# Where the sampling weights' loads stand in SyncE's queue: start of a half band or middle of the one before

## The chip, the cores and the metric

The kernel runs on one core of a Trainium2 chip. The metric is the device time of one execution in microseconds. Before the change the median of three runs was 9661.97 us (9661.39 to 9698.82). A core has five engines with instruction streams of their own: TensorE (PE: matmuls, and PEld for its weight loads), VectorE (DVE), ScalarE (ACT), GpSimd (POOL) and SyncE (SP), which here only issues DMAs. An engine works off its stream in order; a waiting instruction holds up all that follows it on that engine. DMAs are issued by SyncE, by ScalarE's queue and by GpSimd's queue, and run on 16 DMA engines.

## The reference

Thirty-two images of 96 channels by 56 by 56 go through two layers in float32.

- Layer one is an inverted bottleneck: a 1x1 convolution to 576 hidden channels, a 3x3 depthwise convolution, a squeeze-and-excite gate, a 1x1 convolution back to 96, and the input added.
- Layer two computes channel and spatial gates from Fourier magnitudes, multiplies them in (`y`), and then runs a deformable convolution. What matters here is its sampling:

```python
offset = _conv(aux, off_w, off_b, (1, 1))
off = offset.reshape(b, 9, 2, h, w)
px = xx + off[:, :, 0]
py = yy + off[:, :, 1]
sampled = _grid_sample_taps(y, px, py)
y_def = jnp.einsum('bcthw,oct->bohw', sampled, def_w.reshape(c, c, 9))
z = (1 - gate) * y_base + gate * y_def
```

For every pixel and each of nine taps, `_grid_sample_taps` interpolates `y` bilinearly at a fractional place. At the end `z` is normalised over the batch, and `relu(zn + x)` is returned.

## The kernel before

**Tiling.** An image is cut into 7 bands of 8 rows (`NBD`), a band into two half bands of 7 tile pairs (`NTH`). Bilinear sampling is done as a matmul: each 4x4 tile of outputs sees a block of 8x8 = 64 pixels (`NS`), and for each output and tap there is a column of 64 weights, the product of a row hat and a column hat. `block_channels` (line 696) turns the blocks so that pixels lie on partitions; `sample_tiles` (713) multiplies them by the weights (the matmul of line 721, 28 recorded per half band); `pack` (729) and `deform` (735) apply the deformable convolution's own weights.

**The weights' way.** For band n, `offsets` (641) lets TensorE compute the offsets, VectorE copies them to `at` (651), GpSimd's queue stores them as `od` (655), SyncE loads them eight-fold as `ht` (667), ScalarE makes the hats (670, 671), and ScalarE's queue stores them as `hd` in HBM (674). It is a generator of 16 steps spread over one band, two bands ahead of use: `find(n + 2)` runs beside band n, and its store of `hd` is its last step, at that band's end. For each half band `weights_load` (678) then loads from `hd`, with copies, the column hats `wc` and the row hats `wr`: four DMAs of 252 KB each on SyncE (lines 685 and 686, twice). `weights` (690) multiplies them on VectorE in place, 128 x 1008 numbers (line 692): "the product". The pool of `wc` has three buffers, that of `wr` two.

**The main loop** (line 1105) runs over all 224 bands of all images; its half bands are numbered m = 2n + h here. In each half band it

1. issues the loads of half band m + 1 (`prepare`, line 1117; `READY` and `AHEAD` are 1 each, so it asks for loads up to number m + 1),
2. takes the finished weights and blocks of m and samples the first group of three tile pairs,
3. calls `pump()` for each, which moves on two streams of other images: `first` (the bottleneck's hidden layer: taps on VectorE at line 261, xt loads at line 212) and `second` (projection with hq loads at line 305, Fourier magnitudes with x loads at line 361),
4. ends the half band before (`deform`), issues the product of m + 1 (line 1131) and turns blocks,
5. samples the second group of four tile pairs, pumping again, and packs.

At a band's end it pumps three times more and refills rows of `y` (loads of lines 584 and 596).

**What sets the order.** Line 1351 puts SyncE under manual order: it issues its DMAs exactly in the order of the program. For the other engines the framework's planner decides: it reckons when each instruction's inputs will be ready and fills each engine's stream accordingly, earlier program places first. So a changed place of a load in the program changes SyncE's order directly, and may change the planned order of the others.

Of the kernel before, what the change touches and what calls it, by code (L numbers as in the profile page):

```python
# [64 lines left out]
AHEAD = 1  # L65
READY = 1
# [611 lines left out]
def weights_load(nc, p, hd, h):  # L678

    src = hd.rearrange("n i t k -> n i (t k)")[:, :, h * NTH * KP : (h + 1) * NTH * KP]  # L680
    wc = p["wc"].tile([2 * NS, NTH * KP], FP, name="wc")
    wr = p["wr"].tile([2 * NS, NTH * KP], FP, name="wr")
    for s in range(2):
        ps = slice(s * NS, (s + 1) * NS)
        nc.sync.dma_start(wc[ps], src[2 * s].unsqueeze(0).to_broadcast([SB, SB, NTH * KP]))
        nc.sync.dma_start(wr[ps], src[2 * s + 1].unsqueeze(1).to_broadcast([SB, SB, NTH * KP]))
    return wc, wr


def weights(nc, wc, wr):  # L690

    nc.vector.tensor_tensor(wc, wc, wr, ALU.mult)  # L692
    return wc


def block_channels(nc, p, yp, j, h):

    yt = p["yt"].tile([2 * NS, NTH, C], FP, name="yt")
    yb = p["ybl"].tile([C, NTH, 2, SB, SB], FP, name="ybl")
    src = yp[:C, j * RB : j * RB + SB, h * NTH * TS : h * NTH * TS + SB]  # L700
    for s in range(2):
        blocks = bass.AP(src.tensor, src.offset + s * TS * WY, [src.ap[0], [TS, NTH], [WY, SB], [1, SB]])
        nc.gpsimd.tensor_copy(yb[:, :, s], blocks)  # L703
    for lo, hi in ((0, 4), (4, NTH)):
        pt = bank(p)
        for t in range(lo, hi):
            nc.tensor.transpose(pt[:, (t - lo) * C : (t - lo + 1) * C], yb[:, t].rearrange("c s r x -> c (s r x)"),  # L707
                                p["w"]["ident"][:C, :C])
        nc.scalar.copy(yt[:, lo:hi].rearrange("p t c -> p (t c)"), pt[:, : (hi - lo) * C])  # L709
    return yt  # L710


def sample_tiles(nc, p, yt, s, v, group):


    pts = [(bank(p), bank(p)) for _ in group]
    for (lo, hi), pt in zip(group, pts):
        for t in range(lo, hi):
            for k in range(2):
                ps = slice(k * NS, (k + 1) * NS)  # L720
                nc.tensor.matmul(pt[k][:C, (t - lo) * KP : (t - lo + 1) * KP], yt[ps, t], s[ps, t * KP : (t + 1) * KP],  # L721
                                 start=True, stop=True)
    for (lo, hi), pt in zip(group, pts):
        for k in range(2):
            nc.scalar.copy(v[:C, :, lo:hi, k].rearrange("c k t p -> c t k p"),  # L725
                           pt[k][:C, : (hi - lo) * KP].rearrange("c (t k p) -> c t k p", t=hi - lo, k=NTAP))


def pack(nc, v):

    for i in range(3):
        nc.scalar.copy(v[C:, 1 + 2 * i : 3 + 2 * i], v[i * QC : (i + 1) * QC, KA:])  # L732
# [25 lines left out]
def gates_of(nc, p, hid):  # L758

    pgs = bank(p), bank(p)  # L760
    for i, pg in enumerate(pgs):
        ps = slice(i * NS, i * NS + DMID)
        nc.tensor.matmul(pg[:C, :BW], p["w"]["dg2p"][ps], hid[ps], start=True, stop=True)
    return [gate_from(nc, p, pg) for pg in pgs]
# [174 lines left out]
def layers(tc, a, dp, x1d, zd, stats, far):  # L939
# [8 lines left out]
    with ExitStack() as ctx:  # L948
# [29 lines left out]
        def flush():  # L978
            while later:
                later.pop(0)[1]()  # L980
# [27 lines left out]
        def start(b, length):  # L1008
            streams[:] = [[second(b + 1), 0, n_second, slot + 3, slot + length - 8],
                          [first(b + 2), 0, n_first, slot, slot + length]]  # L1010

        def pump():
            nonlocal slot
            slot += 1
            for st in streams:
                due = st[2] * min(1.0, (slot - st[3]) / (st[4] - st[3]))
                while st[1] < due:
                    st[1] += 1
                    next(st[0], None)
            later.sort(key=lambda e: e[0])  # L1020
            while later and later[0][0] <= slot:
                later.pop(0)[1]()

        def drain():
            for st in streams:
                for _ in st[0]:
                    pass
# [3 lines left out]
        def refill(b, upto):  # L1031

            upto = min(H, upto)
            r = filled.get(("y", b), 0)
            while ("sa", b) in p and r < upto:
                r1 = min(upto, r + RB)
                args = load_rows(nc, p, yp, b, x1d[b], r, r1)
                later.append((slot + 4, lambda args=args: attend_rows(nc, p, b, *args)))
                r = filled["y", b] = r1
            r = filled.get(("fq", b), 0)  # L1040
            if ("fq", b) in p and r < upto:
                load_freq(nc, p, yp, b, r, upto)
                filled["fq", b] = upto
# [11 lines left out]
        def end_half(n, h, v, gate, st):  # L1055
            if h == 0:
                pds[n] = p["pd"].tile([128, 512], FP, name="pd")
            deform(nc, p, pds[n], v, h)
            if h:
                pd = pds.pop(n)  # L1060
                later.append((slot + 2, lambda: join(n, pd, gate, st)))
# [14 lines left out]
        def find(n):  # L1076
            if n % 2 == 0:
                hids.append(p["hid"].tile([2 * NS, BW], FP, name="hid"))
            hid = hids[n // 2][n % 2 * NS : n % 2 * NS + DMID]
            return offsets(nc, p, yp, bands[n][1], top[:, n % NBD : n % NBD + 1], hid, ybs, hds)  # L1080
# [11 lines left out]
        def prepare(upto):  # L1092

            nonlocal n_loads
            while n_loads < min(upto, 2 * len(hds)):
                n, m = divmod(n_loads, 2)
                loads.append(weights_load(nc, p, hds[n], m))
                n_loads += 1
# [6 lines left out]
        for n, (b, j) in enumerate(bands):  # L1105
            if j == 0:
                st = p["st"].tile([C, NBD, 6], FP, name="st")
            if j == turn:
                drain()
                refill(b + 1, j * RB - PD)  # L1110
                flush()
                start(b + 1, slots)
            more = find(n + 2) if n + 2 < len(bands) else iter(())
            next(more, None)
            for h in range(2):
                v = p["vp"].tile([128, NTAP, NTH, 2, TP], FP, name="v")
                prepare(2 * n + h + READY + AHEAD)
                s = ready.pop(0)
                yt = yts.pop(0)
                for i, group in enumerate(GROUPS):  # L1120
                    sample_tiles(nc, p, yt, s, v, group)
                    for _ in range(group[0][0], group[-1][1]):
                        next(more, None)
                        pump()
                    if i == 0:
                        for end in ends:
                            end()
                        ends.clear()
                        if h == 1 and n + 1 < len(bands):
                            yts.append(block_channels(nc, p, yp, bands[n + 1][1], 0))  # L1130
                        ready.extend(weights(nc, *ws) for ws in loads[:1])
                        del loads[:1]
                        if h == 0:
                            yts.append(block_channels(nc, p, yp, j, 1))
                pack(nc, v)
                if h == 0:
                    if n % 2 == 0:
                        gates.extend(gates_of(nc, p, hids[n // 2]))
                    gate = gates.pop(0)
                ends.append(lambda n=n, h=h, v=v, gate=gate, st=st: end_half(n, h, v, gate, st))  # L1140
            for _ in more:
                pass
            pump()
            pump()
            pump()
            if b + 1 < B:
                refill(b + 1, (j + 1) * RB - PD if j < NBD - 1 else H)
            if j == NBD - 1:
                nc.vector.tensor_reduce(top[:, NBD:], top, AX.X, ALU.max)
# [350 lines left out]
```

## Time and profile before

| what | value |
|---|---|
| median of the runs | 9661.97 us |
| profiled execution | 9648.5 us (span 9646.7 us) |
| main loop | about 430 to 9358 us of the span, 448 half bands, 19.9 us each |
| TensorE, share busy / granted clock over the span | 88% / 0.923 |
| VectorE, ScalarE, GpSimd busy | 75%, 55%, 26% |
| DMA traffic | 1485.98 MB, 154 GB/s in the mean |
| product of weights (line 692) | 448 times, 1.26 us in the mean |
| loads wc and wr (lines 685, 686) | 896 each, 252 KB each |
| issue of one of these loads on SyncE | 0.57 to 0.60 us |

How to read the profile's lines: a group line gives line number, engine, operation, what it writes and reads, how often, then busy us and the mean in ns, then the idle time of the engine just before these instructions and what ended it. A wait line reads "who <- what it waited for: us in total, times, longest us". The same view for SyncE's queue shows how long the queue stood before an issue. A timeline line gives the start in us, the duration, the engine (a q for an issue by its queue), line, operation, and in brackets the idle time before it with what ended it. A line of busy time by stretch gives the stretch, its length, busy us of PE, PEld, DVE, ACT and POOL with instruction counts, TensorE's granted clock, the DMA engines' busy share, and GB/s.

### The profile page before, as it was taken

What the parts mean: (1) busy time and instruction counts of PE and PEld (TensorE: products, weight loads), DVE (VectorE), ACT (ScalarE), POOL (GpSimd) and SP (SyncE); (2) the same over time, 40 slices, a digit from 0 to 9 for tenths busy, and PEclk for the clock granted to TensorE, in tenths of its full rate; (3) what the DMA queues carried; (4) which work ended last, traced back from release to release, by engine and by line L of the source; (5) the groups of instructions that cost most, each with busy time, mean ns of one, the idle gap of its engine ahead of it and who ended that gap; (6) DMA issues with size and microseconds to landing.
All of it is one profiled execution on the core that took longest, in us unless ns stands there. A gap on an engine that the chain in (4) does not pass through costs nothing. (4 is left out here: it accounts for less than half of the span.)

```text
span 9646.7 us, 129705 instructions
## 1 busy us (share of the span) xinstructions
PE 8472.7 (88%) x48374; PEld 5064.2 (52%) x48374; DVE 7227.2 (75%) x6948; ACT 5322.1 (55%) x10262; POOL 2532.6 (26%) x2642
## 2 busy tenths in 40 slices
PE   6889989998999999999899989999999999999870
PEld 3455555555555555555555555555555555555540
DVE  7688777778777787877777887777878777777323
ACT  2355555565555556555555655555555555565453
POOL 1123223222222322222232322233222323322210
PEclk9899999999999999999999999999999999999985
DMA  2355555555555555555555555555555555554449
GB/s 94 95 143 148 151 152 160 150 149 143 147 155 154 160 154 145 145 149 155 154 160 155 145 142 153 151 158 154 153 139 145 150 157 157 153 152 135 130 154 417
DMA packets 1069473, 1485.98 MB, mean 154 GB/s; under 512 B 590438, under 2 KB 840086, under 8 KB 1056550
## 3 DMA queue, kind: packets, MB, share of 16 engines
q1 hardware_dynamic: 858747, 985.20, 37.9%
q10 hardware_dynamic: 153803, 329.80, 9.2%
q0 software_dynamic: 56288, 162.60, 6.7%
q8 instruction: 388, 6.36, 0.3%
q14 instruction: 247, 2.02, 0.1%
HBM read 1064.29 MB, written 412.65 MB: 153 GB/s over the span
## 5 line engine op out<-in xcount | busy, mean ns | idle before, releaser
L261 DVE SCALAR_TENSOR_TENSOR acch<-hp,w,acch 128x1512 f32<-128x1512 f32 (+1 forms) x2250 | 4320.5, 1920 | 32.8
L605 PE MATMUL mm<-yp,c_jointW 104*128 104x448 f32 x4032 | 1649.0, 561 | 9.0 <-ACT yt L709 5.5
L740 PE MATMUL pd<-v,c_def 128*96 128x224 f32 (+1 forms) x6272 | 1414.8, 376 | 127.6 <-ACT v L732 104.1
L703 POOL COPY ybl<-yp 96x448 f32<-96x448 f32 x896 | 1014.7, 1159 | 1903.7 <-PE mm L707 1903.3
L721 PE MATMUL mm<-wc,yt 64*96 64x144 f32 x12544 | 1168.1, 308 | 153.5 <-DVE yb L638 76.8
L740 PEld LDWEIGHTS pd<-v,c_def 128*96 128x96 f32 (+1 forms) x6272 | 1051.8, 173 | 437.4 <-ACT v L732 142.5
L168 PE MATMUL mm<-xt,w 96*128 96x392 f32 (+3 forms) x2688 | 1136.3, 561 | 133.8 <-ACT yt L709 96.0
L605 PEld LDWEIGHTS mm<-yp,c_jointW 104*128 104x128 f32 x4032 | 783.6, 196 | 806.0 <-issue 762.6
L721 PEld LDWEIGHTS mm<-wc,yt 64*96 64x96 f32 x12544 | 884.2, 167 | 489.8 <-issue 188.0
L221 ACT ACTIVATE acch<-acch,sh,inv 128x1568 f32<-128x1568 f32 x288 | 487.5, 1693 | 1159.0 <-DVE acch L261 1143.9
L692 DVE TENSOR_TENSOR wc<-wc,wr 128x1008 f32<-128x1008 f32 x448 | 564.6, 1260 | 704.2 <-DMA wr<-hd 690.5
L725 ACT COPY v<-mm 96x288 f32<-96x288 f32 (+1 forms) x2688 | 1003.6, 442 | 117.7 <-PE mm L721 78.9
L172 ACT ACTIVATE hp<-mm,sh,inv 128x392 f32<-128x392 f32 (+2 forms) x1216 | 811.8, 672 | 326.9 <-PE mm L168 282.1
L633 PE MATMUL mm<-yp,c_base0W 96*64 96x448 f32 x4032 | 913.5, 550 | 0.0
L323 PE MATMUL mm<-hq,w3s 128*96 128x392 f32 x2048 | 788.2, 531 | 127.4 <-DMA hq<-h2d 125.9
L655 POOL DMA_DIRECT2D od<-at x224 | 186.3, 832 | 2275.1 <-DVE at L651 1451.9
L732 ACT COPY v<-v 32x448 f32<-32x448 f32 x1344 | 755.3, 562 | 30.3
L168 PEld LDWEIGHTS mm<-xt,w 96*128 96x128 f32 (+1 forms) x2688 | 389.9, 189 | 495.1 <-issue 264.8
L709 ACT COPY yt<-mm 128x384 f32<-128x384 f32 (+1 forms) x896 | 350.9, 441 | 491.5 <-PE mm L707 489.4
L323 PEld LDWEIGHTS mm<-hq,w3s 128*96 128x96 f32 x2048 | 336.3, 173 | 477.7 <-issue 382.5
L466 POOL TENSOR_TENSOR o<-o,xc 96x392 f32<-96x392 f32 x256 | 396.5, 1549 | 643.9 <-ACT o L333 642.3
L633 PEld LDWEIGHTS mm<-yp,c_base0W 96*64 96x64 f32 x4032 | 294.6, 134 | 515.5 <-issue 490.2
(194 smaller groups left out, 9023.7 us busy)
## 6 DMA issues: line engine op xcount, KB each, us to landing
h2d<-acch ACTq DMA_DIRECT2D x288, 784.0 KB
wc<-hd SPq DMA_DIRECT2D x896, 252.0 KB
wr<-hd SPq DMA_DIRECT2D x896, 252.0 KB
hq<-h2d SPq DMA_DIRECT2D x128, 980.0 KB
hq<-h2d SPq DMA_DIRECT2D x128, 784.0 KB
x<-x1d SPq DMA_DIRECT2D x768, 98.0 KB
ht<-od SPq DMA_DIRECT2D x224, 252.0 KB
hd<-ht ACTq DMA_DIRECT2D x224, 252.0 KB
```

The lines of the kernel that those rows point to most:

```text
L168: nc.tensor.matmul(pt[p0 : p0 + w1.shape[1], : rows * W], w1, xts[hf][:, r0 * W : (r0 + rows) * W], start=True, stop=True)
L172: nc.scalar.activation(h1[lo:hi, row0 : row0 + rows, 1 : 1 + W], pt[lo:hi, : rows * W].rearrange("p (h w) -> p h w", h=rows), AF.Silu, bia ...
L261: nc.vector.scalar_tensor_tensor(acc[:, lo:hi], win, wk, acc[:, lo:hi], ALU.mult, ALU.add)
L323: nc.tensor.matmul(pts[half][:C, :EW], w3s[:, ch], hq, start=(i == 0), stop=False)
L605: nc.tensor.matmul(view, weights[:, k], yp[:channels, r0 : r0 + RB, dx + PD - 1 : dx + PD - 1 + W], start=(k == 0), stop=(k == NTAP - 1))
L633: nc.tensor.matmul(pb[k % 2 * BC : (k % 2 + 1) * BC, :BW].rearrange("p (h w) -> p h w", h=RB), w["base"][:, k], yp[:C, r0 : r0 + RB, dx + ...
L692: nc.vector.tensor_tensor(wc, wc, wr, ALU.mult)
L703: nc.gpsimd.tensor_copy(yb[:, :, s], blocks)
L721: nc.tensor.matmul(pt[k][:C, (t - lo) * KP : (t - lo + 1) * KP], yt[ps, t], s[ps, t * KP : (t + 1) * KP], start=True, stop=True)
L725: nc.scalar.copy(v[:C, :, lo:hi, k].rearrange("c k t p -> c t k p"), pt[k][:C, : (hi - lo) * KP].rearrange("c (t k p) -> c t k p", t=hi - ...
L732: nc.scalar.copy(v[C:, 1 + 2 * i : 3 + 2 * i], v[i * QC : (i + 1) * QC, KA:])
L740: nc.tensor.matmul(out.rearrange("c q (t x) -> c t q x", x=TS), p["w"]["def"][ks, k], v[ks, k].rearrange("c t s (r x) -> c t (s r) x", r=T ...
```

## The change

The call of `prepare` moves from the start of a half band to its middle, right after the product, and asks for one half band more. At that place in half band m the loads of m + 2 are issued; before, they were issued at the start of half band m + 1. In the program's order the four loads thereby pass what SyncE is given in the second sampling group of m, at the end of a band, and nothing else. The number of loads, their sizes and the buffers are the same; `prepare` still stops at the bands whose `hd` has been written in the program.

```diff
             for h in range(2):
                 v = p["vp"].tile([128, NTAP, NTH, 2, TP], FP, name="v")
-                prepare(2 * n + h + READY + AHEAD)
                 s = ready.pop(0)
                 yt = yts.pop(0)
                 for i, group in enumerate(GROUPS):
@@
                             yts.append(block_channels(nc, p, yp, bands[n + 1][1], 0))
                         ready.extend(weights(nc, *ws) for ws in loads[:1])
                         del loads[:1]
+                        prepare(2 * n + h + 1 + READY + AHEAD)
                         if h == 0:
                             yts.append(block_channels(nc, p, yp, j, 1))
```

## The prediction

> **What bounds the kernel now.** I read the page first (busy shares, costliest groups), then the waits of all engines, the waits of SyncE's own queue, busy time by stretch for the main loop, and the timelines of SyncE, VectorE and TensorE for one image (5019 to 5301 us).
>
> ```profile
> PE 8472.7 (88%) x48374; PEld 5064.2 (52%) x48374; DVE 7227.2 (75%) x6948; ACT 5322.1 (55%) x10262; POOL 2532.6 (26%) x2642
> L692 DVE TENSOR_TENSOR wc<-wc,wr 128x1008 f32<-128x1008 f32 x448 | 564.6, 1260 | 704.2 <-DMA wr<-hd 690.5
> ...
> DVE wc L692 <- DMA wr<-hd: 690.5, 152, 18.3
> PE mm L323 <- DMA hq<-h2d: 125.9, 31, 9.4
> PE mm L386 <- POOL x L366: 34.3, 32, 4.0
> ...
> SPq L361 <- PE mm L386: 1272.9, 144, 52.9
> SPq L667 <- DMA od<-at: 777.1, 83, 15.1
> SPq L685 <- DMA hd<-ht: 702.6, 42, 24.3
> SPq L361 <- DMA x1d<-o: 650.4, 34, 22.0
> ...
> 430.00:9358.00 8928.00, 8172.23 (x47211) 4896.05 (x47209) 6833.02 (x6363) 5105.56 (x9959) 2486.46 (x2576) 0.94 0.54 149
> 5078.00:5111.00 33.00, 24.40 (x123) 14.34 (x117) 20.53 (x18) 16.51 (x34) 2.67 (x2) 0.74 0.36 108
> ```
>
> TensorE bounds the main loop: 8172.2 us busy of 8928, so 755.8 us idle is all that better timing can win, plus what the clock loses (granted 0.94 in the loop, so 0.06 x 8928 = 536 us of clock). VectorE waits 690.5 us for the landing of wr, 152 times, more than for anything else. SyncE's queue spends most of its time waiting: it issues in program order and stands before x loads, ht loads and the weights' loads, so what stands in front of a load sets its time.
>
> The timelines show how (SyncE five lines, VectorE two, TensorE two):
>
> ```profile
> 5033.76 2.82 SPq L361 DMA_DIRECT2D x<-x1d  x6
> 5036.62 0.59 SPq L685 DMA_DIRECT2D wc<-hd  x1
> ...
> 5074.72 0.66 SPq L667 DMA_DIRECT2D ht<-od  x1
> 5075.48 0.57 SPq L685 DMA_DIRECT2D wc<-hd  x1
> 5276.74 9.08 SPq L305 DMA_DIRECT2D hq<-h2d  x2
> ...
> 5047.31 1.21 DVE L692 TENSOR_TENSOR wc<-wc,wr 128x1008 f32<-128x1008 f32 x1 [5.50 <-DMA wr<-hd]
> 5089.44 1.21 DVE L692 TENSOR_TENSOR wc<-wc,wr 128x1008 f32<-128x1008 f32 x1 [8.73 <-DMA wr<-hd]
> ...
> 5091.90 0.74 PE L707 MATMUL mm<-c_ident,ybl 96*128 96x96 f32 x3 [6.19 <-ACT sq L413]
> 5289.26 3.57 PE L323 MATMUL mm<-hq,w3s 128*96 128x392 f32 x7 [3.01 <-DMA hq<-h2d]
> ```
>
> The reader is to see two kinds of late loads. The product at 5047.31 waits for loads that were issued at 5036.62 because six x loads stood before them until 5033.76, waiting for a store of x1d. The product at 5089.44 waits for loads issued at 5075.48 behind an ht load that waited for od; TensorE then idles 6.19 us, released over ScalarE's squares and VectorE.
>
> **The change, part by part.**
>
> *What moves.* Nothing is added or removed: 448 sets of four loads, 0.57 to 0.60 us each to issue, 2.5 us a set. The set for half band m goes from the start of half band m-1 to the middle of m-2, right after the product for m-1. On SyncE it passes just what the streams and the refill issue in the second sampling group: by the program's order some 662 x loads (L361), 180 hq loads (L305), 248 yp loads and 93 frequency rows (L584, L596) and 58 xt loads (L212), over the whole run. It does not pass the ht load (L667), which is issued in the first group. The POOL and ScalarE queues keep their issues.
>
> *Gain on VectorE.* In the image shown the products wait 5.5 (5047.31), 8.7 (5089.44), 5.5 (5240.1) and 2.0 us (5286.0), 21.7 in all; 690.5 / 32 images is 21.6, so it is typical. Before three of the four stand x or hq loads, which the set now passes; there it can be issued 13 to 20 us sooner than before (from the queue's last issue before its new place, and from hd's landing), more than the stall. Before the fourth (8.7) stands the ht load: that stall stays. So 13.0 of 21.7, 60% or about 414 us of VectorE's waits, go.
>
> *What of it reaches TensorE.* I followed each TensorE gap of the loop back over its releasers to the last TensorE instruction: 304 us (155 gaps) pass a landing of wr. 184 us of these are in the fourth half band of the images (the 6.19 us is one), behind the stall that stays. 120 us are elsewhere. Those cannot give more than 120, and give nothing if the ScalarE copies that release TensorE next (rows L725, L732, L709 in its waits) are as late. I take 85: next late are those copies, and they queue behind VectorE's work only in part.
>
> *Clock.* Idle TensorE costs clock beside: 536 us lost for 755.8 idle, 0.7 us per us; in the stretch 5078 to 5111 8.6 us idle and a clock of 0.74. The gaps that go are shorter than that one, so I take half of 0.7: 85 x 0.35 = 30, bounds 0 and 60. [...]
>
> *Cost: who stands behind the set now.* A set that must wait holds SyncE. Sets for even m need hd, stored by ScalarE near the end of the band before (landing 2.6 us after its issue where SyncE waited for it). One place per image gets a hold of some 23 us: the set at 5105.39 already waits for hd, and the xt load before it (5081.81) will now stand behind. I cost this at nothing: xt is loaded some 100 us before its use, and TensorE waited for xt only at the kernel's start (33.2 us); without that cover it would be up to 23 us per image. Elsewhere hd holds the queue 0 to 3 us. x loads behind the set come 2.5 us later and share its transfer; TensorE and POOL wait little for x now (34.3 us, and 17.9 for x's landing): I take +15, bounds 0 and +52, a doubling. The waits on buffers are not new: wc of m is free when m-3 was sampled, wr when product m-2 ran, both before the new place but for one place per image where hd holds longer anyway and one with 4.5 us.
>
> *hq.* The last hq quarter makes TensorE wait 125.9 us. The load issued at 5276.74 lands 12.5 us later, with a set (5271.1 to 5273.7) in front of it; after the change that set has gone 13 us earlier. But the next set is then issued between the two hq loads (5277 and 5285.5), and the second lands later. Bounds -126 and +256 (8 us in each of 32 images); the two pull opposite ways, I take 0.
>
> *Order on the other engines.* Only SyncE follows the program; for the others a planner, which reckons when data land, sets the order, and it will plan anew. The trace cannot show this. Bounds: -60 (a third of the 184 us behind the stall that stays) and one more stall like that of 5089.44 per image, 6.2 us x 31 = +192 without clock. I take +20, near the small end, since in most half bands VectorE is over 85% busy (17.96 of 18 us in the half band at 5204) and leaves little room to move a product.
>
> *Sum.* -85 - 30 + 15 + 0 + 20 = -80 us. The profiled execution took 9648.5 us (span 9646.7), so 9568; the median of the runs, 9661.97, is 13.5 above the profiled one, so 9582.
>
> **The rivals.**
>
> *A. Forecast:* the stalls at x and hq loads go, 9582 (0.8% faster), its own range 9480 to 9613. For it: nothing but SyncE's waiting loads stood before those sets.
>
> *B. The stall moves with the product (slower).* The planner sees the loads land sooner and puts the product as much earlier on VectorE; where it reckons the landing too early, VectorE stands again. For it: that happened in the fourth half band, where the product ran half a half band ahead of its place in the program, 11.3 us after its last load was issued, and stalled 8.7. Against: in most half bands VectorE is too full. Price: one more such place per image, 6.2 us of TensorE plus 0.7 of it in clock = 10.5 us x 31 = 326, less the 80 won: 9908; in half of the images: 9745. It decides from about 2.6 us of new TensorE idle per image on (80 / 31), if the products' lead falls below 12 us. [...]
>
> *C. The second hq load of the last quarter is late (slower).* Set between the hq loads: +256 - 126 + the -80 above = +50, 9710. It decides if that hq load lands over 6 us later than now. Against: the set may have landed by then.
>
> *D. No change.* VectorE's stalls go, but TensorE waits as long for the ScalarE copies: 0 reaches it, costs +15 + 20: 9697, range 9615 to 9710. For it: TensorE's idle rows name ScalarE in the main, VectorE's product itself 7.7 us.
>
> **How the numbers follow.** A measurement of this kernel can tell about 0.5% from no change (48 us; the runs span 37). A 0.50, B 0.16, C 0.13, D 0.21. Faster by over 0.5%: A but for its edge, 0.48. Within: D and edges, 0.22. Slower: B, C, 0.30. The predicted time is A's, 9582. The range: down to 9430 (the full 120 with 60 of clock, and half of hq's 126: 9419, rounded in), up to 9800 (C, and B in up to two thirds of the images); beyond lie the rest of B and a planner's luck.
>
> **What the changed profile would show.** Right: VectorE's wait for wr at 250 to 320 us, most of it in the fourth half band; the sets behind x and hq loads 13 us or more sooner; TensorE idle in the loop near 670 us; clock 0.94 to 0.95. B: that wait at 500 us or more, products earlier than now against the sampling that uses them. C: the row of L323 waiting for hq over 200 us. D: wr's row down and TensorE's idle still about 750. What would make it wrong above all: a new order on ScalarE or VectorE that delays the copies TensorE waits for, which no row of this trace shows.

## The result and the profile after

The changed kernel takes 9817.83 us in the median (9809.00 to 9838.04) against 9676.99 us of the kernel before beside it: a ratio of 1.0147, 95% interval 1.0117 to 1.0177, some 142 us slower. 9582 was predicted, and the measured time lies above the range's upper end, 9800. Of these last 18 us, 15 are the base's: the median of the kernel before was 9661.97 over three runs and 9676.99 with the fourth. The profiled execution took 9838.04 us (span 9836.2).

From the page of the changed kernel (busy time, and the group of the product):

```profile
PE 8601.3 (87%) x48374; PEld 5139.0 (52%) x48374; DVE 7286.7 (74%) x6948; ACT 5325.8 (54%) x10264; POOL 2446.4 (25%) x2642
...
L692 DVE TENSOR_TENSOR wc<-wc,wr 128x1008 f32<-128x1008 f32 x448 | 563.5, 1258 | 738.8 <-DMA wr<-hd 726.5
```

From the waits of its engines (us in total, times, longest us):

```profile
DVE wc L692 <- DMA wr<-hd: 726.5, 221, 18.8
...
ACT yb L628 <- DVE at L651: 434.5, 129, 9.0
...
PE mm L721 <- DVE yb L638: 192.1, 89, 6.7
...
PE mm L386 <- POOL x L366: 171.2, 57, 7.9
...
PE mm L323 <- DMA hq<-h2d: 12.8, 6, 7.2
```

In the kernel before, ScalarE's wait for VectorE's `at` was:

```profile
ACT yb L628 <- DVE at L651: 128.0, 70, 5.2
```

From the waits of the changed kernel's SyncE queue:

```profile
SPq L685 <- DMA hd<-ht: 1566.2, 131, 27.3
...
SPq L361 <- DMA x1d<-o: 316.6, 30, 14.0
```

And the changed kernel's busy time over the main loop:

```profile
430.00:9545.00 9115.00, 8297.47 (x47188) 4969.92 (x47186) 6892.63 (x6362) 5107.76 (x9958) 2400.73 (x2576) 0.92 0.54 146
```

The stall that was to go has not gone: the product waits 726.5 us for wr instead of 690.5, and 221 times instead of 152. The hq wait is gone (125.9 to 12.8). SyncE waits less behind x1d (650.4 to 316.6) and more than twice as long for hd (702.6 to 1566.2). TensorE's idle time in the loop is 9115.00 - 8297.47 = 817.5 us, 62 more than before, and its busy time has grown by 125 at a lower clock (0.94 to 0.92).

What happened is plainest in one half band, the eleventh of an image (number 10, counted 0 to 13). VectorE, ScalarE and TensorE of the changed kernel, from its timelines (brackets: idle before, and what ended it):

```profile
5627.85 1.21 DVE L692 TENSOR_TENSOR wc<-wc,wr 128x1008 f32<-128x1008 f32 x1 [4.13 <-DMA wr<-hd]
5629.10 0.69 DVE L651 COPY at<-mm 18x224 f32<-18x224 f32 x2
...
5629.82 0.63 ACT L628 ACTIVATE yb<-mm,c_cvec 32x448 f32<-32x448 f32 x1 [3.62 <-DVE at L651]
...
5630.50 0.48 PE L721 MATMUL mm<-wc,yt 64*96 64x144 f32 x2 [0.38 <-ACT yb L628]
5631.25 0.73 PE L721 MATMUL mm<-wc,yt 64*96 64x144 f32 x6 [0.27 <-ACT hp L172]
5632.42 0.73 PE L721 MATMUL mm<-wc,yt 64*96 64x144 f32 x8 [0.44 <-DVE yb L638]
```

The same place in the kernel before:

```profile
5501.54 1.21 DVE L692 TENSOR_TENSOR wc<-wc,wr 128x1008 f32<-128x1008 f32 x1 [1.01 <-DMA wr<-hd]
5502.78 0.69 DVE L651 COPY at<-mm 18x224 f32<-18x224 f32 x2
...
5506.69 1.22 PE L721 MATMUL mm<-wc,yt 64*96 64x144 f32 x16
```

Before, the product here was that of half band 11. In the changed kernel it is already that of half band 12, one half band further ahead: its loads were issued from 5615.19 to 5617.14, the sampling that uses it starts at 5657.13, and yet it stands and waits 4.13 us. Behind it on VectorE queues `at` (651), behind that ScalarE's `yb` (628), behind that TensorE's sampling, which stands three times, 1.1 us in all. This half band took 13.5 us here and 11.5 before; in the mean over 29 images (the third to the 31st) it takes 15.1 against 10.9. The planner has moved the products forward as far as the loads. In the mean over 29 images, the product of half band 2 / 10 / 12 ended 14.4 / 12.8 / 12.5 us before its use, and now 34.2 / 31.6 / 30.5; from the last load's issue to the product it was 11.0 / 12.2 / 9.6 us and is 8.2 / 8.2 / 10.1.

It is not only the products. Counting the instructions outside the longest run common to both orders, the planner moved 1111 of 6836 instructions on VectorE, 314 on ScalarE, 112 on TensorE, 69 on GpSimd. So a run that changes SyncE's order in this kernel changes two things at once, and the experiments had to part them.

### The profile page after: what moved, and what is told of

The parts are those of the page before. It is cut to its first block, busy times and chain, and to the rows that moved or that the text cites. A ratio compares the mean times of both kernels' runs of the same rounds, so it can differ in the third digit from the quotient of the medians.

```text
span 9836.2 us, 129699 instructions
## 1 busy us (share of the span) xinstructions
PE 8601.3 (87%) x48374; PEld 5139.0 (52%) x48374; DVE 7286.7 (74%) x6948; ACT 5325.8 (54%) x10264; POOL 2446.4 (25%) x2642
## 3 DMA queue, kind: packets, MB, share of 16 engines
q14 instruction: 247, 2.02, 0.1%
## 5 line engine op out<-in xcount | busy, mean ns | idle before, releaser
L261 DVE SCALAR_TENSOR_TENSOR acch<-hp,w,acch 128x1512 f32<-128x1512 f32 (+1 forms) x2250 | 4368.8, 1942 | 32.9
L740 PE MATMUL pd<-v,c_def 128*96 128x224 f32 (+1 forms) x6272 | 1487.2, 388 | 93.4 <-ACT v L732 63.1
L703 POOL COPY ybl<-yp 96x448 f32<-96x448 f32 x896 | 926.6, 1061 | 2112.2 <-PE mm L707 2110.9
L721 PE MATMUL mm<-wc,yt 64*96 64x144 f32 x12544 | 1219.6, 316 | 265.3 <-DVE yb L638 192.1
L740 PEld LDWEIGHTS pd<-v,c_def 128*96 128x96 f32 (+1 forms) x6272 | 1090.8, 180 | 451.7 <-ACT v L732 113.8
L721 PEld LDWEIGHTS mm<-wc,yt 64*96 64x96 f32 x12544 | 921.3, 172 | 628.4 <-DVE yb L638 219.1
L692 DVE TENSOR_TENSOR wc<-wc,wr 128x1008 f32<-128x1008 f32 x448 | 563.5, 1258 | 738.8 <-DMA wr<-hd 726.5
L323 PE MATMUL mm<-hq,w3s 128*96 128x392 f32 x2048 | 735.0, 502 | 15.8 <-DMA hq<-h2d 12.8
L386 PE MATMUL mm<-c_FU,x 112*128 112x116 f32 x3072 | 462.9, 298 | 188.9 <-POOL x L366 171.2
L386 PEld LDWEIGHTS mm<-c_FU,x 112*128 112x128 f32 x3072 | 421.0, 207 | 317.7 <-POOL x L366 209.9
L259 DVE TENSOR_SCALAR acch<-hp,w 128x1568 f32<-128x1568 f32 x270 | 284.8, 1055 | 401.6 <-ACT hp L172 400.6
```

The lines of the kernel that those rows point to most:

```text
L261: nc.vector.scalar_tensor_tensor(acc[:, lo:hi], win, wk, acc[:, lo:hi], ALU.mult, ALU.add)
L323: nc.tensor.matmul(pts[half][:C, :EW], w3s[:, ch], hq, start=(i == 0), stop=False)
L386: nc.tensor.matmul(pt[:, i * 4 * V : (i + 1) * 4 * V], x2s[g][:, 2 * i : 2 * i + 2, :].rearrange("h c w -> h (c w)"), w["FU"], start=True, ...
L740: nc.tensor.matmul(out.rearrange("c q (t x) -> c t q x", x=TS), p["w"]["def"][ks, k], v[ks, k].rearrange("c t s (r x) -> c t (s r) x", r=T ...
```

## The experiments

All runs are in one table. "Old order" means that the four engines other than SyncE are held to the order that the planner gave the kernel before, instruction by instruction; "new order" that of the changed kernel. Waits are those of the profiled execution in us: the product for wr; TensorE's sampling for VectorE's `yb` (638); TensorE for x (386).

| run | loads moved | order of the other engines | median us | ratio to before (95%) | wr | yb | x |
|---|---|---|---|---|---|---|---|
| before | none | planned | 9655 to 9677 | 1 | 690.5 | 76.8 | 34.3 |
| after | all | planned | 9817.8 | 1.0147 (1.0117 to 1.0177) | 726.5 | 192.1 | 171.2 |
| e1 | all | planned, product pinned | 9628.6 | 0.9978 (0.9964 to 0.9993) | 186.5 | 176.0 | 142.3 |
| e2 | none | planned, product pinned | 9458.6 | 0.9788 (0.9772 to 0.9804) | 414.9 | 66.1 | 61.5 |
| e3 | all, no wait for hd | planned (23 instructions off the new order) | 9643.2 | 0.9988 (0.9975 to 1.0001) | 604.7 | 154.1 | 181.8 |
| e4 | all but 8, 9 | planned | 9850.1 | 1.0200 (1.0173 to 1.0227) | 800.1 | 263.9 | 54.0 |
| e5 | all but 1 | planned | 9841.6 | 1.0177 (1.0160 to 1.0194) | 744.4 | 170.1 | 173.3 |
| e6 | 0 alone | planned, product pinned | 9335.1 | 0.9646 (0.9630 to 0.9662) | 318.7 | 153.2 | 61.6 |
| e7 | 0 alone | planned | 9595.3 | 0.9921 (0.9902 to 0.9940) | 781.0 | 221.3 | 34.1 |
| e8 | all but 1, 8, 9, 10, 12 | planned, product pinned | 9617.8 | 0.9935 (0.9919 to 0.9952) | 152.0 | 176.6 | 58.7 |
| e9 | all | old order | 9607.3 | 0.9935 (0.9913 to 0.9957) | 203.3 | 222.2 | 87.4 |
| e10 | none | new order | 12455.2 | 1.2894 (1.2860 to 1.2927) | 3782.5 | 474.3 | 42.0 |
| e11 | none, no wait for hd | old order | 9650.1 | 0.9981 (0.9968 to 0.9995) | 703.5 | 66.5 | 33.9 |
| e12 | all, no wait for hd | old order | 9590.1 | 0.9913 (0.9881 to 0.9946) | 172.0 | 232.4 | 84.8 |
| e13 | all | that of e2 | 9516.5 | 0.9840 (0.9814 to 0.9865) | 20.1 | 172.3 | 119.6 |
| e14 | all | new order, products where they were before | 9623.2 | 0.9960 (0.9946 to 0.9975) | 214.8 | 176.2 | 107.5 |
| e15 | all | old order, products where the new order has them | 9884.1 | 1.0217 (1.0195 to 1.0240) | 722.5 | 245.4 | 63.6 |
| e16 | all but 8, 9, 10 | that of e2 | 9457.0 | 0.9783 (0.9767 to 0.9799) | 37.2 | 185.3 | 60.2 |

"Loads moved: all but 8, 9" names the half bands of each image whose sets stay at the old place. In e3, e11 and e12 the even half bands are sampled with the weights of the band before, which are long stored; the amount of work is the same. Below, the time of a half band runs from its first sampling matmul (line 721) to the next one's, in the mean over the same 29 images; differences between kernels go by the ratios, each to the kernel before run beside it.

### Holding the product at its place in the program (e1, e2)

```diff
-def weights(nc, wc, wr):
+def weights(nc, p, wc, wr):
-    nc.vector.tensor_tensor(wc, wc, wr, ALU.mult)
+    p["tc"].keep_in_program_order(nc.vector.tensor_tensor(wc, wc, wr, ALU.mult))
```

The pin puts the product on VectorE behind all that the program has issued there before it. The first is the changed kernel with it, the second the kernel before with it.

> The changed kernel with one thing more: the product of line 692 is pinned behind the VectorE instruction before it in the program, so that the planner cannot put it forward. Theory P (the planner moved the product forward with its loads, so the stall came along): VectorE's wait for wr falls from 726.5 us below 200 us, the gaps in the first, eleventh and twelfth half band of an image go (4.0 + 4.2 + 1.6 us x 32 = 314 us over the change), only the eighth stays long; time 9350 to 9600 us, faster than before the change. Rival Q (SyncE is held by the sets that wait for hd, and x loads come late behind them): the pin alters nothing of that; time 9750 us or more.

> The kernel before with the same pin on the product and the loads at their old place. Theory P: the product in the fourth half band, which was put forward by half a half band and stalled 8.7 us, goes back; VectorE's wait for wr falls from 690 to some 350 us, since the sets behind x and hq loads are as late as before; time 9400 to 9680 us. It says what the pin alone does. Rival Q makes no difference here: 9677 us as before.

The pin takes 0.0169 (163 us) off the changed kernel, but 0.0212 (205 us) off the kernel before as well: most of that falls in the fourth half band, the place of the old stall (28.6 to 21.4 us in e2). So a product put forward too far seems dear in both kernels; this pair alone doesn't show it, since from the kernel before to e2 637 VectorE, 534 ScalarE and 784 TensorE instructions changed place. e1 lies between its two forecasts: the wait for wr fell as far as the first asked (186.5), the time did not (9629). Between the two pinned kernels the moved loads still cost 0.0190 (183 us; 170 in the medians). Is that SyncE's queue? Not shown by this pair either: the planner moved 710 VectorE instructions between them.

### No wait for hd, sets put back one by one (e3, e4, e5)

```diff
-                loads.append(weights_load(nc, p, hds[n], m))
+                loads.append(weights_load(nc, p, hds[n if m else max(0, n - 1)], m))
```

```diff
                 v = p["vp"].tile([128, NTAP, NTH, 2, TP], FP, name="v")
+                if (2 * n + h + 1) % 14 in (8, 9):
+                    prepare(2 * n + h + READY + AHEAD)
...
-                        prepare(2 * n + h + 1 + READY + AHEAD)
+                        if (2 * n + h + 2) % 14 not in (8, 9):
+                            prepare(2 * n + h + 1 + READY + AHEAD)
```

The first edit is e3's, the second e4's; e5's is the same with half band 1 alone in place of 8 and 9.

> The changed kernel, but the first half band of each band loads its weights from the hd of the band before, long stored, so that no set waits for hd; the sampled values of those half bands are therefore those of other offsets, the work is the same. Rival Q: SyncE's wait for hd (1566 us) goes, the loads behind come earlier and the time falls to 9680 us or less. Theory P: sets for even half bands land still earlier and the planner puts the products as much earlier again; VectorE still waits over 500 us for wr; time 9760 to 9880 us.

> The changed kernel with two of an image's fourteen sets (for the ninth and tenth half band) issued at the old place, behind the x loads. If the eighth half band is longer (27.0 to 31.2 us) because its x loads come behind those sets, it goes back to some 27 us, TensorE's wait for POOL's x (171 us) falls below 60 us, and the time to 9818 - 4.2 x 32 = 9684 us. If it is longer by the new order of the products, it stays at 31 us and 9818 us. Theories P and Q both leave the other half bands as they are.

> The changed kernel with one set of each image (the second half band's) issued at its old place again. Half bands of an image are counted 0 to 13 here, and half band 0 went from 18.8 to 22.8 us with the change. SyncE theory: the set issued in half band 13 stands before the loads of y's rows (yp, L584), these land late, and VectorE's yp (L592) and the chain behind it hold TensorE; with the set back, half band 0 falls to about 19 us, VectorE's wait for x1d's rows from 61 to about 28 us, and the kernel gains 4.0 x 31 = 124 us on the changed one: ratio to the kernel before about 1.002. Planner theory: half band 0 is slow because the planned order there is another; then one set's return changes it little or by chance, half band 0 stays over 21.5 us, and the ratio is 1.010 to 1.018.

Without the wait for hd the changed kernel loses its whole disadvantage, and the planner's order is the same but for 23 instructions. That looked like the cause: SyncE held by hd. The two others spoke against a tale of SyncE's queue alone. In e4 half band 7 fell from 31.2 to 26.5 us, but half bands 8 and 10 gave it back (16.0 to 19.4, 15.1 to 16.2). In e5 half band 0 fell from 22.8 to 20.0, and 1 to 3 gave that back. Each time the planner had shifted 150 and 332 VectorE instructions.

### One set alone, and five sets back (e6, e7, e8)

The edit is the condition above: only the set of half band 0 moved (e6 with the pin, e7 without it), and with the pin all but the sets of 1, 8, 9, 10 and 12 (e8).

> The kernel before with the product held at its place in the program, and of 14 sets of an image only one moved, that of half band 0: it then stands in front of nothing but the last hq load. With the product held and no set moved, half band 13 took 28.7 us; with the product held and all moved 23.0. If what the move wins lies in this set alone, half band 13 falls to about 23.0 us, TensorE's wait for hq from 125 to under 20 us, and the kernel is 5.7 x 31 = 177 us faster than the one with the product held: about 9280 us, ratio 0.960 to the kernel before. Rival: the gain of half band 13 needs the other moved sets, or is given back in half bands 0 and 1 through the loads of y's rows: then 9400 to 9460, ratio 0.974 to 0.979.

> The kernel before with only the set of half band 0 moved, the product free to be planned. If the planner's answer is local (a product is put forward where its own loads are), the 13 other half bands stay as before and half band 13 wins 5.7 to 5.9 us: 9655 - 180 = 9475, ratio 0.981. If one moved set makes the planner shift the rest of the image, or the gain of half band 13 rests on the other sets, the ratio is above 0.990.

> The changed kernel with the product held at its place, and the sets of half bands 1, 8, 9, 10 and 12 of each image at their old places: those that stand before the loads of y's rows, before the last x loads of the spatial gate, or that wait for hd while other loads stand behind. Against the kernel with product held and all sets moved (9629), SyncE theory: half bands 0, 7, 10 and 11 fall by 3.9, 5.7, 2.8 and 1.1 us, half band 8 gives back 1.8: 11.7 x 31 = 363 less, about 9270, ratio 0.960. Rival: the loss moves on to the other half bands, as it did when two sets alone were put back: 9460 or more, ratio 0.979 or more.

Between e2 and e6 the planner's order is nearly the same (32 VectorE instructions, 2 on ScalarE, 3 on TensorE), so e6 shows what one moved set does: half band 13 falls from 28.7 to 23.1 us, since the set no longer stands before the last hq load (TensorE's wait for hq falls from 124.6 to 6.3), and half band 0 gives back 3.3 (19.0 to 22.3). An image is 3.3 us shorter in the profiled executions; by the ratios 0.0142 (137 us) remain, between the two forecasts. In e7, with the planner free, the gain is smaller: half band 13 falls by 5.5, half band 0 rises by 5.6. In every run whose set 0 has moved, TensorE's wait for `yb` is 153 us or more; in the runs without it and with timely loads it is 66 to 77. e8 missed its forecast by 350 us: half bands 7, 8 and 11 came out within 0.4 us of the forecast, 10 within 1.0, but half band 0 fell by 1.7 in place of 3.9, and half band 9 took 30.1 us in place of 20.1 in e6, with 6.97 us of TensorE idle an image before the matmuls of line 284, which wait for ScalarE's `acch` (221); there the planner had built yet another order (591 VectorE and 150 TensorE instructions off that of e6).

### Both orders, crossed (e9, e10)

Here the other four engines' orders are written into the kernel: the order in which the instructions of one kernel stand on each engine is read from its built program and imposed on the other kernel with edges of order alone, which are to add no wait between engines. Imposing the old order on the kernel before costs nothing that shows: e11 below does so, with one wait of SyncE less, and lies at 0.9981.

```diff
+def replay(tc):
...
+    for engine, packed in ORDER.items():
+        mine = [i for i in traced if i.engine == engine and type(i).__name__.startswith("Inst")]
+        place = np.frombuffer(zlib.decompress(base64.b85decode(packed)), np.int16).cumsum(dtype=np.int64)
+        for a, b in zip(place, place[1:]):
+            tc.add_manual_dep(mine[b], mine[a].name, mybir.DependencyInfo(
+                mybir.DependencyClass.NoSync, mybir.DependencyReason.DATA), reason="replay")
...
         layers(tc, a, dp, x1d, zd, stats, far)
+        replay(tc)
```

> The changed kernel's SyncE order (all sets moved), while TensorE, VectorE, ScalarE and GpSimd are held, instruction by instruction, to the order that the planner gave the kernel before. Only the loads' places differ from the kernel before. Theory S (the loss lies in SyncE's queue: sets that wait for hd, and sets in front of other loads): the loss stays whole, ratio 1.010 to 1.018. Theory P (the loss comes from the new order that the planner gave the other engines): the products stay where they were, their loads are 13 to 20 us sooner, VectorE's wait for wr falls from 690 to 350 us or less, and the ratio is 0.98 to 0.995. A mixture would lie at 1.000 to 1.008.

> The other corner: SyncE's order of the kernel before, the other four engines held to the order that the planner gave the changed kernel. Theory P: the order itself is the loss, so the time stays at 1.015 or rises, since the products now stand up to half a half band earlier while their loads come as late as before: VectorE's wait for wr over 1000 us, ratio 1.02 to 1.05. Theory S: the order does little, and without the sets standing in front of x, yp and hd the time falls back to 0.995 to 1.010 in spite of the later loads.

With e9's waits of the engines,

```profile
PE mm L721 <- DVE yb L638: 222.2, 72, 7.2
...
DVE wc L692 <- DMA wr<-hd: 203.3, 50, 10.9
...
PE mm L386 <- POOL x L366: 87.4, 36, 4.6
...
PE mm L323 <- DMA hq<-h2d: 23.7, 11, 7.5
```

its SyncE queue,

```profile
SPq L685 <- DMA hd<-ht: 1600.8, 132, 25.9
```

its main loop,

```profile
430.00:9345.00 8915.00, 8186.69 (x47203) 4911.77 (x47202) 6859.81 (x6362) 5095.95 (x9958) 2589.67 (x2576) 0.93 0.56 150
```

and e10's waits,

```profile
DVE wc L692 <- DMA wr<-hd: 3782.5, 330, 30.8
...
PE mm L721 <- DVE yb L638: 474.3, 64, 25.6
```

the two causes come apart. The moved loads by themselves make the kernel faster, by 0.0065 of 9662 us = 63 us (42 to 84), although SyncE waits for hd as long as in the changed kernel (1600.8). The planner's new order costs the difference to 1.0147: 0.0212 of 9662 = 205 us. With the loads where they were, that order is ruinous: 12455 us, a ratio of 1.2894 where at most 1.05 was forecast. It was planned for loads that come early; with late ones VectorE stands 3782.5 us for wr.

At the place shown above, e9's VectorE and TensorE:

```profile
5512.75 1.19 DVE L692 TENSOR_TENSOR wc<-wc,wr 128x1008 f32<-128x1008 f32 x1
5514.53 0.69 DVE L651 COPY at<-mm 18x224 f32<-18x224 f32 x2 [0.59 <-ACT hid L625]
...
5519.73 1.22 PE L721 MATMUL mm<-wc,yt 64*96 64x144 f32 x16
```

The product is again that of half band 11, with loads issued by 5491.91, 21 us earlier, and TensorE samples without a gap.

Half band by half band, an image of the changed kernel is 6.6 us longer than one of e9: 4.2 at number 10, 3.5 at 7 (where TensorE waits for x), 1.6 at 11, less 2.1 at 8; the others add up to 0.6 less.

### Is the hold by hd dear by itself? (e11, e12)

The edit of e3, on the kernel before and on e9.

> The control for the run without a wait for hd: the kernel before, order of the other engines held, sets of even half bands loaded from the previous band's hd (so their offsets are the previous band's; the amount of work is the same). In the changed kernel this took 174 us away at an unchanged order of the other engines. If the hold of SyncE by hd is what the move made worse (SyncE's wait for hd 702.6 us before, 1566.2 after), it gives the kernel before less than half of that: ratio 0.990 to 1.000. If the kernel before gains 174 us as well (ratio 0.982), the hold is as dear without the move and does not explain the loss.

> All sets moved, the order of the other engines held to that of the kernel before, and no wait for hd (even half bands sampled with the previous band's offsets). What is left is the early loads alone. Theory S: the prediction's gain appears, 0.980 to 0.990, and the difference to the same kernel with the wait is 100 to 200 us. Theory P: the hold matters little at this order, the difference is under 60 us.

At the old order the wait for hd costs 0.0022 of 9662 = 21 us with the loads moved (9607.3 to 9590.1 in the medians, the intervals overlap) and 18 us with the loads unmoved (0.9981). At the new order the same edit took away 0.0159 = 154 us (e3). So the hold is not dear because the loads moved; it is dear in the new order. Of the 6.3 us an image that e3 wins, 5.1 lie in half bands 10 and 11, where e14 below, which keeps the hold and puts the products back, wins 5.7; this points to products that had no time left to bear the hold. This corrects what e3 alone had suggested.

### The products' place or the rest of the order? (e14, e15)

The orders of e9 and the changed kernel are mixed: in e14 the 448 products alone are put back on VectorE behind the instruction behind which they stood in the kernel before; in e15 they alone are put forward. In both, 368 products change place and nothing else does.

> The changed kernel with the order that the planner gave it held on all four engines, but for the 448 products: each stands on VectorE behind the instruction behind which it stood in the kernel before (368 of them move). Theory P1 (the new order is dear because it puts the products forward to where their loads are late): about all of the 205 us between the changed kernel and the one with the old order held goes, ratio 0.990 to 1.000, VectorE's wait for wr under 250 us. Theory P2 (the products' place is not what is dear, but the other 740 shifted VectorE and 435 shifted ScalarE instructions): ratio 1.008 to 1.016.

> The mirror of the run before it: all sets moved, the order of the kernel before held, but for the products, which stand on VectorE where the planner put them in the changed kernel. Theory P1: the loss is back, ratio 1.010 to 1.022, wait for wr 600 us or more. Theory P2: the ratio stays near that of the old order held (0.9935), at most 1.002.

The waits of e14,

```profile
DVE wc L692 <- DMA wr<-hd: 214.8, 50, 11.5
...
PE mm L721 <- DVE yb L638: 176.2, 62, 7.1
```

and of e15:

```profile
DVE wc L692 <- DMA wr<-hd: 722.5, 224, 18.6
...
ACT yb L628 <- DVE at L651: 509.3, 131, 11.5
...
PE mm L721 <- DVE yb L638: 245.4, 99, 7.3
```

Moving 368 products and nothing else takes 0.0187 (181 us) off the changed kernel, and lays 0.0282 (272 us) on the kernel with the old order. Half band 10, the one shown above, falls from 15.1 to 10.9 us in e14 and rises from 10.9 to 15.6 in e15. The rest of the new order, 744 VectorE and 314 ScalarE instructions (435 in the expectation), costs next to nothing with the products at their old places (e14 and e9 differ by 0.0025); with the products forward it is even worth 0.0070 (e15 against the changed kernel), and why is open. The products' new places are the loss.

The way from the wait to TensorE can be summed as the prediction did it. TensorE gaps that go back to a landing of wr take 304 us in the kernel before, 147 in e9, 448 in the changed kernel, 196 in e14 and 375 in e15.

### What is left of SyncE's queue (e13, e16)

> All sets moved, the order of the other engines held to that of the kernel before with the product pinned (9459 us with unmoved loads). When all sets were moved and the planner was free but for the product, the time was 9629. If these 170 us came from the planner's new order of the other work, this run takes 9400 to 9460, ratio 0.972 to 0.979; if they came from the loads' places in SyncE's queue, it stays near 9629, ratio 0.993 to 0.998.

> As the run before it, with the sets of half bands 8, 9 and 10 of each image at their old places. With the old order held and all sets moved, half bands 7, 8 and 9 took 0.7, 1.9 and 0.8 us more than in the kernel before: these sets stand before the last x loads and before others while they wait for hd. If that is the price of these sets, this run is 3.4 x 31 = 105 us faster than the one with all sets moved, and below the best so far (9335); if the price is smaller, it is within 40 us of it.

The waits of e13:

```profile
PE mm L721 <- DVE yb L638: 172.3, 44, 7.2
...
PE mm L386 <- POOL x L366: 119.6, 21, 7.9
...
DVE wc L692 <- DMA wr<-hd: 20.1, 6, 7.9
```

e13 lies between its two forecasts. e1 and e2 lie 0.0190 apart; by e13, 0.0138 of it (133 us) came from the planner's order, and 0.0052 (50 us) are the loads' own. Here VectorE hardly ever waits for wr any more (20.1 us against 414.9 in e2), and yet the kernel is slower than e2: half band 13 is 5.6 us shorter, but half bands 0 and 7 are 4.5 and 3.7 us longer, with longer waits for `yb` (66.1 to 172.3) and x (61.5 to 119.6). e16 shows the x part: with sets 8, 9 and 10 back, the x wait is 60.2 again, half band 7 falls from 32.6 to 28.4, half band 9 gives 2.3 back, and 59 us are won; 105 was forecast, and it is not below e6.

The best kernel of the study is e6, 9335 us, ratio 0.9646: the product pinned, one set of an image moved.

## Why the prediction was wrong

**Which step failed.** The term "Order on the other engines" of the sum, taken as +20 within -60 and +192. It measured +205 (e9 against the changed kernel). Its working called VectorE too full ("over 85% busy" in "most half bands") to leave "room to move a product". That was misread: in the busy times by stretch of the image shown (5019 to 5301 us), VectorE is over 85% busy in 7 of 14 half bands, and in number 10, where the loss is largest, it was busy 4.63 of 11 us:

```profile
5222.00:5233.00 11.00, 10.98 (x73) 5.78 (x71) 4.63 (x8) 9.03 (x18) 2.42 (x4) 1.00 0.76 254
```

The planner moved 368 of 448 products, and e14 and e15 show that these moves alone are worth 181 and 272 us. Without this term the sum was -100; e9 measured -63 (-42 to -84).

**Rival B was what happened.** It was given 0.16. Its mechanism, place and condition hold: the products run earlier against the sampling that uses them, the stall goes with them (wr 726.5, it asked for 500 or more), the lead from the last load's issue lies at 8 to 10 us for eight of an image's 14 products, where four did before (it asked for under 12), and TensorE's idle time over e9 is 817.5 - 728.3 = 89 us, 2.8 an image (it decides from 2.6). That this lies so near the rival's figure is partly luck: half band 10 adds 1.5 us, half band 7 2.5 in waits for x, and others give some back. e14 and e15 show the cause by moving the products alone. Its price of 326 for new stalls in all images was too high and that for half of them too low (9908 and 9745; measured 9818).

**The other terms, as e9 shows them at the old order.** Its profiled execution (9637.65) was the slowest of its five runs, 30 us above their median, so its idle and busy times are rather high.

- *Gain on VectorE*, 414 us of stalls: 690.5 - 203.3 = 487 went. The stall behind the ht load, which was to stay, was halved (5.8 to 3.0 us in the mean for that product).
- *What of it reaches TensorE*, 85 us: following each TensorE gap back as before, 147 us pass a landing of wr, against 304. So 157 us of such gaps went, more than the 120 that the step allowed. But the idle time of the loop fell by only 755.8 - 728.3 = 27.5 us, because two other waits of TensorE grew, those for x and for `yb`.
- *x loads*, +15 within 0 and +52: TensorE's wait for x rose from 34.3 to 87.4, +53, the upper bound.
- *A term that was missing*: TensorE's wait for VectorE's `yb` at the start of an image, 76.8 to 222.2, +145. Half band 13 is 5.9 us shorter without the hq wait, half band 0 then 5.4 us longer (18.8 to 24.2). VectorE's `at` and, behind it, `yb` are not ready sooner.
- *hq*, 0 within -126 and +256: the wait fell by 102, and the second hq load was not late (rival C did not happen). Net of half band 0 little is left, so 0 was near, for a reason that the step did not have.
- *Hold by hd*, costed at nothing: right at the old order (e11, e12), 154 us at the new one (e3).
- *Clock*, -30: no gain; TensorE's busy time in the loop rose by 14 us. The records show a granted clock of 0.50 for 34.6 us an image before and 36.0 in e9: 3.3 less in half band 3 and 4.4 less in 13, but 4.6 more in 0. That the gaps that go would win half of 0.7 us of clock per us was the author's estimate; e9 does not show it.

**What the profile had shown.** The stall at 5089.44, taken as the exception that stays, was the rule of the planner: a product put half a half band ahead of its place, at a load it reckoned to have landed. e2, which has no such stall in the fourth half band, is 205 us faster than the kernel before, though its pin moved other work too. The prediction drew rival B from that line and then held it down to 0.16, because VectorE was "too full". Both e9 and the changed kernel issue the loads early: e9, which waits for them where the wait was, gains 63 us, and the changed kernel, which waits early too, loses 142.

**What stays open.** Why one set's move makes VectorE late at the start of an image, beyond that `at` is late there, was not taken apart; nor which of the sets 1 to 7 and 11 to 13 costs the rest of what lies between e16 and e6 (0.0137, 132 us). Nor was it taken apart how the products' places lengthen TensorE's wait for x in half band 7: with the new order it falls from 171.2 to 107.5 us when they are put back, with the old order it falls too, from 87.4 to 63.6, when they are put forward.

## What to carry to other kernels

Where a planner sets the engines' order, an earlier load is also an earlier consumer: pin the consumer where it is wanted, or hold the old order, before judging the load's new place. Crossing the two orders (new loads with old order, old loads with new order) tells which of them pays, and putting one group of instructions back names the culprit. And a wait counts by what queues behind it: 20 us of waiting for wr in one kernel and 415 in another stood beside times that differed the other way.

## What was not expected of the hardware

- The loss grows by TensorE's clock. From e9 to the changed kernel TensorE idles 89 us more in the loop and is busy 8297.47 - 8186.69 = 111 us longer with the same work, at a granted clock of 0.92 in place of 0.93: 1.2 us of clock for each us idle, where 0.7 was taken from the mean of the kernel before. The clock records agree: a granted clock of 0.50 for 44.0 us an image in place of 36.0. In e10, where TensorE idles some 94 us an image in place of some 23, the records show a granted clock of 0.50 for 129.8 us an image in place of 34.6, and the granted clock of the whole run is 0.822.
- In half band 10 of the changed kernel the clock fell beside little idle time. TensorE idles 1.5 us an image there, where before it idled 0.02, in no image longer than 2.02 us at a stretch or 2.4 us in all, and in 24 of 29 images the granted clock falls to 0.50, for 4.7 us in the mean over the 29; in the kernel before it did so in none. In one image two gaps of 1.59 and 0.27 us are followed by 10.2 us at a granted clock of 0.50 (from 2162.7 us on), and the half band takes 17.6 us in place of 11.5.
- VectorE's largest wait was worth little in itself. From the kernel before to e9 it fell by 487 us and the kernel gained 63.
